# A residual block on one core: the last image's second results stay in SBUF for the last stage, and the involution's constant part is split in two

## The chip, the cores and the metric

The kernel runs on one core of a Trainium2 chip. The metric is device time in microseconds of one execution, the median of several. A profile is one further execution recorded by the hardware profiler. It gives the span from the first to the last instruction of the program, each instruction's start and end, and what the DMA engines moved. Five engines work side by side: TensorE (PE; PEld is its weight load), VectorE (DVE), ScalarE (ACT), GpSimd (POOL) and SyncE (SP). SP and ACT both issue DMA transfers here, SP the loads and most stores, ACT the stores of the output. Each of them takes its instructions in order.

## The reference

The input x has 8 images of 256 channels and 56 x 56 pixels in float32. Two residual layers follow each other:

```
x = x + involution(groupnorm(x))      # 7x7 kernels made from the image itself, 16 groups
y = groupnorm(x)
y1 = conv3x3(y, t(w1)) + conv1x1(y, centre of t(w1))    # t(): weights rounded to -1, 0, 1
r1 = relu(batchnorm(y1))              # mean and variance over all 8 images
y2 = conv3x3(r1, t(w2)) + conv1x1(r1, centre of t(w2))
out = x + relu(r1 + batchnorm(y2))
```

Both batch norms need sums over all images, so each convolution must be complete before the next step can use its result.

## The kernel before, in words

**Involution.** An image is cut into four quarters of 64 channels, 32 quarters in all, and a quarter into ten rows (`TY`), nine of three pixel lines and a last shorter one. While `apply_row` (L905) multiplies the rows of one quarter with its matrices of kernels, `generate` makes the matrices of the next quarter, in 14 units (`UNITS`, L867): TensorE into PSUM, then ScalarE (L871) and VectorE (L881) into SBUF with a bias. `PER_ROW` (L63) says how many steps of the generator follow each row. After the units, `constant` (L819 to L848) adds the part that the group norm's shift contributes: for each of the three pixel lines of a row (`py` 0, 1, 2) and for the last, shorter row (`py` = `PY`, which uses the same reduced image `kr[0]` as line 0) matmuls with summed weights (L832), one activation (L840) and one addition onto x (L847, on GpSimd). It has two steps, of lines (0, 1) and of (2, last row), and both stand in row 8. GpSimd also adds each row's result onto x (L922) and fills the rims of the loaded patches `q` two rows ahead (L797). `reduce` (L759) makes `kr` for the next image in the rows that `STRIPS` names, of the third and fourth quarter. `pin()` holds each engine to the order of the text in this stage. x after the involution goes to DRAM (`x1_d`).

**Convolutions.** `conv_phase` runs twice, over 16 half images. Each half image is transformed along its rows into six planes, split into a high and a low part; TensorE multiplies the planes in the order 1, 2, 3, 4, 0, 5 (`ORDER`, L561) and VectorE combines the results into the half image `y` (tile of two buffers, 12,544 bytes in each partition), whose sums are taken by ScalarE (L491). `y` is stored to DRAM (`y1_d`, then `y2_d`, L605 to L607). The last half image's sums are taken piece by piece so that the batch norm's scale and shift (L186 to L205) follow TensorE's end closely. The weights of planes 1 to 4 lie in the pool `wqa`, those of 0 and 5 in `wqb`.

**Last stage.** 16 tiles (8 images, two tiles of 128 channels), L1152 to L1165. For each tile y1, y2 and x1 are loaded from DRAM by SP (L1160), ScalarE normalizes y1 (L1161), VectorE adds the scaled y2 (L1162), ScalarE applies the relu (L1163), VectorE adds to x1 (L1164) and ACT's queue stores to the output (L1165). The last two tiles go in 2 and 4 parts. The loads may begin before the second convolution has ended, where their memory has been given up. Their memory is four pools, each of which begins where the convolutions' pools lay: y1 and y2 have two buffers each, x1 three, and a pool holds up to three of them. Apart from the involution, the order on an engine comes from a scheduler, which works from the text, the pools and its own estimates.

Of the kernel before, what the change touches and what calls it, by code (L numbers as in the profile page):

```python
# [8 lines left out]
F32 = mybir.dt.float32  # L9
F32R = mybir.dt.float32r  # L10
# [5 lines left out]
SBUF = bass.MemoryType.SB  # L16
# [43 lines left out]

FIRST = (1, 4, 7, 10)

PER_ROW = (2, 2, 2, 1, 2, 2, 1, 2, 2, 0)  # L63
NQB = 5
PLEAD = 2
RIM_AT = 1
# [19 lines left out]
QS = WT  # L86
SLOT = (0, 2, 3, 4, 5, 1)
QM, QM2 = 6, 12


@with_exitstack
def involution_tri_block_kernel(
# [256 lines left out]

    def weights(i, k):  # L350

        w = (wqb if k in ORDER[4:] else wqa).tile([P, CT, 3, C], F32R, tag=f"wq{k}",
                                                  name=f"wq{i}_{k}")
        n = CT * 3 * C
        nc.sync.dma_start(w.rearrange("p t k o -> p (t k o)").bitcast(F32),
                          wq_d[i - 1][:, SLOT[k] * n:(SLOT[k] + 1) * n])
        return w
# [9 lines left out]
            raws.append(raw)  # L367
        return raws

    def conv_phase(i, begun, src_d, norm, stats, shift, dst_d, follow):  # L370

# [154 lines left out]
        for n in range(2 * B):  # L528
            b, h = n // 2, n % 2
            cur, nxt = nxt, {}  # L530
            more = n + 1 < 2 * B
            steps = transform(n + 1, raws, nxt) if more else iter(())
            next(steps, None)
            final = n == 2 * B - 1
            if n + 2 < 2 * B:
                raws = load(i, n + 2, src_d)
            elif not final and follow:
                begun = {}, load(i + 1, 0, dst_d)
            y = wk.tile([P, CT, NH], F32, tag="y", bufs=2, name=f"y{i}_{n}")
            yr = [y.rearrange("p o (r k w) -> p o k r w", k=4, w=W)[:, :, k] for k in range(4)]  # L540

            def row_of(k, x, c, z, op):
                for to in range(CT):
                    nc.vector.scalar_tensor_tensor(yr[k][:, to], x[:, to], c, z[:, to],
                                                   ALU.mult, op)

            def half(name):
                return wk.tile([P, CT, HT, W], F32, tag=name, name=f"{name}{i}_{n}")

            m = {}  # L550
            for k in ORDER:
                ps = ps_c.tile([P, CT, 512], F32, tag="conv", name=f"c{i}_{n}_{k}")
                steps_ = [(to, part, t) for to in range(CT) for part in cur[k] for t in range(CT)]
                if n == 0 and k == 1:
                    steps_ = [(to, part, t) for t in range(CT) for to in range(CT)
                              for part in cur[k]]
                count, last = [0] * CT, CT * 3 * 2 - 1
                for to, part, t in steps_:
                    for dx in range(3):
                        c = count[to]  # L560
                        nc.tensor.matmul(  # L561
                            ps[:, to, :NM], wq[k][:, t, dx, to * P:(to + 1) * P],
                            part[:, t, :, dx:dx + W], start=(c == 0), stop=(c == last))
                        count[to] += 1
                if final and follow:
                    begun[0][k] = weights(i + 1, k)
                m[k] = ps[:, :, :NM].rearrange("p o (r w) -> p o r w", w=W)
                next(done, None)
                if k in (2, 4):
                    e = half("e")  # L570
                    nc.scalar.copy(e, m[k])
                if k == 2:
                    s, d = half("s"), half("d")
                    nc.vector.tensor_tensor(s, m[1], e, ALU.add)
                    nc.vector.tensor_tensor(d, m[1], e, ALU.subtract)
                elif k == 4:

                    s2, d2 = half("s2"), half("d2")
                    nc.vector.tensor_tensor(s2, m[3], e, ALU.add)
                    nc.vector.tensor_tensor(d2, m[3], e, ALU.subtract)  # L580
                    nc.vector.tensor_tensor(yr[1], d2, d, ALU.subtract)  # L581
                    row_of(2, s2, 2.0, s, ALU.subtract)
                    for z, z2, c in ((s, s2, 0.5), (d, d2, 4.0)):
                        flat, flat2 = (v.rearrange("p o r w -> p (o r w)") for v in (z, z2))
                        nc.vector.scalar_tensor_tensor(flat, flat2, c, flat,
                                                       ALU.mult, ALU.subtract)
                    if final:
                        last_rows(n, y, 1, 2)
                elif k == 0:
                    row_of(0, m[0], 1.5, s, ALU.add)  # L590
                    if final:
                        moments = half("s2").rearrange("p o r w -> p o (r w)")[
                            :, :, :18].rearrange("p o (n s) -> p o n s", s=6)
                        row_stats(moments, y, 0, 0)
                elif k == 5:
                    if final:
                        batch_norm_before(stats, total)
                    row_of(3, m[5], 6.0, d, ALU.add)
                    if final:
                        row_stats(moments, y, 3, 1)  # L600
                        row_sums(moments)
                next(steps, None)
            for _ in steps:
                pass
            for to in range(CT):  # L605
                (nc.scalar if final else nc.sync).dma_start(
                    dst_d[b][to][:, h * NH:(h + 1) * NH], y[:, to])  # L607
            done = statistics(n, y)
        return begun, total

# [9 lines left out]
    with ExitStack() as ph1:  # L620
# [198 lines left out]
        def constant(b, c):  # L819
# [1 line left out]
            n = (TY - 1) * TX  # L821
            xv = xs[b, c][:, :(TY - 1) * PY * W].rearrange("p (t y w) -> p y t w", y=PY, w=W)
            scale, bias = prm[b][0][:, c, 1:2], prm[b][2][:, c:c + 1]
            for i0 in (0, 2):
                ps = ps_pair(f"ks_{b}_{c}_{i0}")
                add = work.tile([P, 2 * PX * n], F32, tag="add", name=f"add_{b}_{c}_{i0}")
                for i in range(2):
                    py = (i0 + i) % PY
                    k0, m = (0, n) if i0 + i < PY else (NT, TX)
                    rows = slice(i * CR, (i + 1) * CR)  # L830
                    for h in range(2):
                        nc.tensor.matmul(ps[i][h * CH:(h + 1) * CH, :PX * m], wsx[rows, c, :],  # L832
                                         kr[py][rows, :, k0 + h * m:k0 + (h + 1) * m],
                                         start=True, stop=True)
                for i in range(2):
                    py = i0 + i
                    m = n if py < PY else TX
                    v = add[:, i * PX * n:i * PX * n + PX * m].rearrange(
                        "p (t w) -> p t w", w=W)
# [10 lines left out]
        def generate(b, c, a, shared=()):  # L850

            whole, rest = (v.rearrange("q t (g p) -> q g p t", g=GQ) for v in views(a))
            for u, (gp, p0, n) in enumerate(UNITS):
                ps = ps_pair(f"pg_{b}_{c}_{u}")
                nt = NT + (NE if p0 < PX else 0)
# [25 lines left out]
                        ps[0][:NQ, t0 * n:t1 * n].rearrange("q (t p) -> q t p", p=n),  # L883
                        bt[:, c, g, p0:p0 + n].unsqueeze(1).to_broadcast([NQ, t1 - t0, n]), ALU.add)
                yield
            yield from constant(b, c)

        def apply_row(b, c, a, ty):

# [207 lines left out]

    with ExitStack() as ph2:  # L1100
        rawp, wqa, wqb, pad, tmpp, planes, wk, ps_c = (
            ph2.enter_context(tc.tile_pool(name=name, bufs=bufs, space=space))
            for name, bufs, space in (
                ("rawp", 1, SBUF), ("wqa", 1, SBUF), ("wqb", 1, SBUF), ("pad", 1, SBUF),
                ("tmpp", 1, SBUF),
                ("planes", 8, SBUF), ("wk", 1, SBUF), ("ps_c", 4, PSUM)))

# [11 lines left out]

        xp = pad.tile([P, 4, CT, HT + 1, WP], F32, tag="xp", name="xp")  # L1120
        nc.gpsimd.memset(xp.rearrange("p f t r w -> p (f t r) w")[:, :, ::WP - 1], 0.0)
        begun, total = conv_phase(1, begun, x1_d, norm_x1, st1, nc1, y1_d, True)

# [7 lines left out]
                nc.vector.tensor_scalar(dst, src, scale, bias, ALU.mult, ALU.add)  # L1133
                nc.vector.tensor_scalar(dst, dst, 0.0, None, ALU.max)

        _, total = conv_phase(2, begun, y1_d, norm_y1, st2, nc2, y2_d, False)

    sc2, bi2 = batch_norm_params(total, nc2, g2_sb, b2_sb, "bn2")  # L1140
    with ExitStack() as ph4:

        fa, fb, fc, fd = (ph4.enter_context(tc.tile_pool(name=name, bufs=1))
                          for name in ("fa", "fb", "fc", "fd"))
        homes = {"y1": (fd, fa), "y2": (fd, fb), "x1": (fd, fb, fc)}

        def home(name, j):
            k = j % len(homes[name])
            return homes[name][k].tile([P, HW], F32, tag=f"{name}{k}", name=f"{name}f_{j}")


        for j in range(B * CT):  # L1152
            b, t = j // CT, j % CT
            y1f, y2f, x1f = (home(name, j) for name in ("y1", "y2", "x1"))
            n = {B * CT - 2: 2, B * CT - 1: 4}.get(j, 1)
            f = HW // n
            for cols in (slice(k * f, (k + 1) * f) for k in range(n)):
                y1, y2, x1 = y1f[:, cols], y2f[:, cols], x1f[:, cols]
                for v, src in ((y1, y1_d), (y2, y2_d), (x1, x1_d)):
                    nc.sync.dma_start(v, src[b][t][:, cols])  # L1160
                nc.scalar.activation(y1, y1, AF.Relu, bias=bi1[:, t:t + 1], scale=sc1[:, t:t + 1])  # L1161
                nc.vector.scalar_tensor_tensor(y1, y2, sc2[:, t:t + 1], y1, ALU.mult, ALU.add)  # L1162
                nc.scalar.activation(y1, y1, AF.Relu, bias=bi2[:, t:t + 1])  # L1163
# [88 lines left out]
```

## Time and profile before

| what | us |
|---|---|
| median of three runs | 2143.46 (2142.48 to 2144.44) |
| profiled execution, its own time | 2144.3 |
| its span | 2142.5 |
| involution, 58 to 1035 us of the span | 977 |
| first convolution, 1035 to 1478 | 443 |
| second convolution, 1478 to 1908 | 430 |
| after TensorE's end, 1908 to 2142.5 | 234.5 |
| TensorE busy over the span | 1750.4 (82%) |
| VectorE busy over the span | 1760.6 (82%) |
| ScalarE busy over the span | 1428.7 (67%) |
| GpSimd busy over the span | 584.1 (27%) |

The stages' limits are read from the times at which TensorE's lines change. A busy share over the whole span mixes stages of different kinds, so the prediction reads each stage by itself. In a group of instructions the last column gives the idle time of the engine just before them and what ended it; in the DMA view a queue's bytes and the mean rate count.

### The profile page before, as it was taken

Reading aid. Unit: us, or ns where it says so; the run is one execution under the profiler, and the core shown is the slowest. Engines: PE = TensorE matmul, PEld = TensorE weight load, DVE = VectorE, ACT = ScalarE, POOL = GpSimd, SP = SyncE. Lnnn points to the kernel's source line nnn. Section 1 sums busy time; section 2 is a strip of 40 time slices with the busy share of each in tenths; the row PEclk is TensorE's granted clock in tenths of the full one; section 3 lists DMA queues with packets and bytes.
Section 4 is the critical chain, followed back from the end, with each engine's and each line's share of the span. In section 5 each row is a group of like instructions: output and inputs, shape, how many; then the busy total and the mean of one; then the engine's idle time right before and its main releaser. Section 6 shows DMA issues by size and latency. Waiting matters only on the chain.

```text
span 2142.5 us, 70728 instructions
## 1 busy us (share of the span) xinstructions
PE 1750.4 (82%) x29680; PEld 1621.5 (76%) x29680; DVE 1760.6 (82%) x3360; ACT 1428.7 (67%) x3537; POOL 584.1 (27%) x960
## 2 busy tenths in 40 slices
PE   5898898989898897988799999998999999960000
PEld 5787777868777686877799999998999999950000
DVE  6778879787777878777899999998999999984444
ACT  4877787877778687777466666665676666653343
POOL 1655566555655555565000000000000000000000
PEclk9999999999999899999899999999999999985555
DMA  5767677686757768677633333335333333369999
GB/s 186 235 181 235 208 237 237 198 254 199 254 180 245 223 179 254 180 205 210 235 123 123 123 123 123 123 123 203 112 139 125 120 126 123 122 270 428 430 429 393
DMA packets 155370, 440.06 MB, mean 205 GB/s; under 512 B 63006, under 2 KB 73116, under 8 KB 147628
## 3 DMA queue, kind: packets, MB, share of 16 engines
q1 hardware_dynamic: 149760, 403.89, 55.2%
q10 hardware_dynamic: 5004, 31.56, 3.5%
q8 instruction: 235, 3.85, 0.7%
q14 instruction: 83, 0.68, 0.1%
q0 software_dynamic: 288, 0.08, 0.0%
HBM read 323.28 MB, written 112.20 MB: 203 GB/s over the span
## 4 chain that ended last, share of the span: by engine, by line
PE 69%; DVE 11%; DMA 9%; issue 5%; ACT 4%; POOL 1%; SPq 0%; ACTq 0%; POOLq 0%; DVEq 0%
PE c L561 39%; PE pg L867 15%; PE pa L905 9%; PE pk L759 4%; DMA y1f<-y1d 3%; DMA x1f<-x1d 2%; ACT a L871 2%; PE ks L832 2%; DMA out_y<-x1f 2%; DMA y2f<-y2d 1%; DVE inv L917 1%; DVE x1f L1164 1%; DVE a L881 1%; DVE st L153 1%; ACT add L840 1%
## 5 line engine op out<-in xcount | busy, mean ns | idle before, releaser
L561 PE MATMUL c<-pl,wq 128*128 128x392 f32 x4608 | 858.0, 349 | 11.3 <-ACT pl L433 9.2
L561 PEld LDWEIGHTS c<-pl,wq 128*128 128x128 f32 x4608 | 855.1, 190 | 13.9 <-ACT pl L433 9.6
L871 ACT ACTIVATE a<-pg,bt 126x126 f32<-126x126 f32 x2028 | 524.8, 457 | 110.8 <-PE pg L867 110.5
L867 PE MATMUL pg<-kr,wl 64*126 64x140 f32 (+1 forms) x6144 | 456.3, 291 | 43.2 <-ACT a L871 17.3
L867 PEld LDWEIGHTS pg<-kr,wl 64*126 64x126 f32 x6144 | 395.3, 194 | 72.7 <-issue 28.5
L905 PE MATMUL pa<-a,q 126*32 126x48 f32 x17024 | 289.0, 215 | 63.7 <-issue 55.6
L905 PEld LDWEIGHTS pa<-a,q 126*32 126x32 f32 x17024 | 241.1, 116 | 128.9 <-issue 86.8
L881 DVE TENSOR_TENSOR a<-pg,bt 126x504 f32<-126x504 f32 (+4 forms) x640 | 280.8, 481 | 37.4 <-PE pg L867 35.9
L922 POOL TENSOR_TENSOR x<-x,inv 128x168 f32<-128x168 f32 x310 | 161.1, 520 | 394.9 <-DVE inv L917 355.4
L917 DVE SCALAR_TENSOR_TENSOR inv<-pa,gn1s,inv 128x168 f32<-128x168 f32 (+1 forms) x384 | 134.0, 351 | 156.3 <-ACT inv L915 153.4
L410 ACT CAST pl<-r 128x812 fp32r<-128x812 f32 x190 | 160.7, 868 | 130.8 <-DVE r L405 121.5
L386 POOL MEMSET xp<- 128x116 f32 x32 | 6.3, 196 | 828.4 <-DVE a L405 805.1
L797 POOL TENSOR_TENSOR q<-q,sides 126x256 f32<-126x256 f32 (+1 forms) x320 | 225.7, 706 | 7.8 <-DMA q<-in_x_nb 7.8
L411 DVE TENSOR_TENSOR pl<-r,pl 128x812 fp32r<-128x812 f32 x190 | 185.3, 1002 | 28.0 <-ACT pl L410 26.7
L491 ACT ACTIVATE dummy<-y,nc 128x1568 f32<-128x1568 f32 (+1 forms) x128 | 200.2, 1564 | 4.8 <-DVE y L581 3.5
L915 ACT ACTIVATE inv<-pa,gn1s 128x168 f32<-128x168 f32 x320 | 133.3, 417 | 62.8 <-PE pa L905 47.6
L153 DVE BATCH_NORM_STATS2 st<-x 128x6 f32<-128x392 f32 x256 | 138.0, 555 | 7.9 <-DMA x<-in_x 7.4
L847 POOL TENSOR_TENSOR x<-x,add 128x504 f32<-128x504 f32 x124 | 123.2, 1024 | 12.6 <-ACT add L840 12.6
L1131 ACT ACTIVATE xp<-raw,bi_bn,sc_bn 128x392 f32<-128x392 f32 (+1 forms) x125 | 83.0, 721 | 60.3 <-DVE a L405 58.9
L1111 ACT ACTIVATE xp<-raw,gn 128x392 f32<-128x392 f32 (+1 forms) x125 | 83.3, 721 | 52.7 <-DVE a L405 51.6
L1162 DVE SCALAR_TENSOR_TENSOR y1f<-y2f,sc_bn,y1f 128x3136 f32<-128x3136 f32 (+2 forms) x20 | 56.6, 2831 | 62.8 <-DMA y2f<-y2d 52.5
L759 PE MATMUL pk<-x,wrn 64*128 64x168 f32 (+1 forms) x1152 | 101.8, 317 | 0.1
(186 smaller groups left out, 1812.0 us busy)
## 6 DMA issues: line engine op xcount, KB each, us to landing
q<-in_x_nb SPq DMA_DIRECT2D x320, 448.0 KB, 4.2
raw<-x1d SPq DMA_DIRECT2D x32, 812.0 KB, 7.0
raw<-y1d SPq DMA_DIRECT2D x32, 812.0 KB, 5.9
x1d<-x SPq DMA_DIRECT2D x64, 392.0 KB, 5.2
x<-in_x SPq DMA_DIRECT2D x60, 392.0 KB, 5.2
y1d<-y SPq DMA_DIRECT2D x30, 784.0 KB, 3.3
y2d<-y SPq DMA_DIRECT2D x30, 784.0 KB, 3.8
y1f<-y1d SPq DMA_DIRECT2D x14, 1568.0 KB, 15.1
```

The costliest lines, as they stand in the source:

```text
L153: nc.vector.bn_stats(st[:, j, :], xt[:, j * NC:(j + 1) * NC])
L410: nc.scalar.copy(hi, r)
L411: nc.vector.tensor_tensor(lo, r, hi.bitcast(F32), ALU.subtract)
L491: nc.scalar.activation(dst, v, f, bias=shift[:, to:to + 1], accum_out=stats[:, to, j, n:n + 1])
L561: nc.tensor.matmul(ps[:, to, :NM], wq[k][:, t, dx, to * P:(to + 1) * P], part[:, t, :, dx:dx + W], start=(c == 0), stop=(c == last))
L759: nc.tensor.matmul(ps[h][:, :m * W], wrn[rows, c, :], src[rows, r0:r0 + (m - 1) * PY + 1:PY, :], start=(c == 0), stop=(c == NCQ - 1))
L797: nc.gpsimd.tensor_tensor(v, v, z, ALU.add)
L867: nc.tensor.matmul(dst, wl[rows, c, gp, o:o + NQ], kr[py][rows, px, :], start=True, stop=True)
L871: nc.scalar.activation(dst[:, g + 1, p0 + j], ps[1][:NQ, j * nt + t0:j * nt + t1], AF.Identity, bias=bt[:, c, g + 1, p0 + j:p0 + j + 1])
L881: nc.vector.tensor_tensor(dst[:, g, p0:p0 + n].rearrange("q p t -> q t p"), ps[0][:NQ, t0 * n:t1 * n].rearrange("q (t p) -> q t p", p=n), ...
L905: nc.tensor.matmul(ps[o:o + m, k * w:(k + 1) * w], q[:NQ, k, o:o + m], av[:, t + k, g * w:(g + 1) * w], start=True, stop=True)
L922: engine.tensor_tensor(xv, xv, iv.rearrange("p t (y x) -> p y t x", x=PX), ALU.add)
```

## The change

Five edits, in two places of the program.

- **Second results that stay.** `conv_phase` gets an argument `stays`. In the second convolution the two half images of the last image are not stored; their tiles `y` are kept. So that they outlive the convolution's pools, `y` moves to a pool `keep` on the other side of SBUF, opened ahead of the convolutions.
- **The last stage opens with the last image.** Tile j belongs to image (j / 2 - 1) mod 8. Tiles 0 and 1 take y2 from the kept half images, in two parts each, and load y1 and x1 alone. Ten loads are written ahead of the loop, in the order of `FIRST_LOADS`.
- **Pools of the last stage.** Eleven pools, one to a tile: four buffers for y1, two for y2, four for x1, and one spacer (`SPACE`), so that each tile lies over few of the convolution's pools. y1's first buffer lies over none of them.
- **Weights in three pools**, of two planes each in the order of use: 1 and 2, 3 and 4, 0 and 5.
- **The constant part in two halves.** The pairs are now (0, last row) and (1, 2). The first stands after the sixth unit (`CONST_AT`), in row 3; the second stays in row 8. `PER_ROW` changes so that row 3 has no unit and row 6 has two.

In the built program SP issues y1 tile 0's load at the start of the second convolution, between the weight loads and the raw loads of half image 1. The order of the next loads on SP is y1 tile 1, x1 tile 1, y1 tile 2, x1 tile 0, y2 tiles 2 and 3, x1 tile 2, y1 tile 3, x1 tile 3. ScalarE's first activations of y1 tiles 0 and 1 stand inside the second convolution, and that of y1 tile 2 ahead of the last four sums.

```diff
-PER_ROW = (2, 2, 2, 1, 2, 2, 1, 2, 2, 0)
+PER_ROW = (2, 2, 2, 1, 2, 2, 2, 2, 1, 0)
+CONST_AT = 5
...
+FIRST_LOADS = [("y1", 0), ("y1", 1), ("x1", 1), ("x1", 0), ("y1", 2), ("y2", 2), ("y2", 3),
+               ("x1", 2), ("y1", 3), ("x1", 3)]
...
-        w = (wqb if k in ORDER[4:] else wqa).tile([P, CT, 3, C], F32R, tag=f"wq{k}",
+        w = wqs[ORDER.index(k) // 2].tile([P, CT, 3, C], F32R, tag=f"wq{k}",
...
-            y = wk.tile([P, CT, NH], F32, tag="y", bufs=2, name=f"y{i}_{n}")
+            y = keep.tile([P, CT, NH], F32, tag="y", bufs=2, name=f"y{i}_{n}")
...
-            for to in range(CT):
-                (nc.scalar if final else nc.sync).dma_start(
-                    dst_d[b][to][:, h * NH:(h + 1) * NH], y[:, to])
+            if stays is not None and b == B - 1:
+                stays.append(y)
+            else:
+                for to in range(CT):
+                    (nc.scalar if final else nc.sync).dma_start(
+                        dst_d[b][to][:, h * NH:(h + 1) * NH], y[:, to])
...
-            for i0 in (0, 2):
+            for pair in ((0, PY), (1, 2)):
...
+            made = constant(b, c)
             for u, (gp, p0, n) in enumerate(UNITS):
...
                 yield
-            yield from constant(b, c)
+                if u == CONST_AT:
+                    next(made)
+                    yield
+            yield from made
...
+    keep = ctx.enter_context(tc.tile_pool(name="keep", bufs=1, side="right"))
...
-        fa, fb, fc, fd = (ph4.enter_context(tc.tile_pool(name=name, bufs=1))
-                          for name in ("fa", "fb", "fc", "fd"))
-        homes = {"y1": (fd, fa), "y2": (fd, fb), "x1": (fd, fb, fc)}
+        h = [ph4.enter_context(tc.tile_pool(name=f"f{i}", bufs=1)) for i in range(11)]
+        h[9].tile([P, SPACE], F32, tag="space2", name="space2")
+        homes = {"y1": (h[10], h[0], h[4], h[7]), "y2": (h[6], h[2]),
+                 "x1": (h[5], h[1], h[3], h[8])}
...
+        for name, j in FIRST_LOADS:
+            tail_load(name, j)
         for j in range(B * CT):
-            b, t = j // CT, j % CT
...
+            b, t = (j // CT - 1) % B, j % CT
+            n = parts_of.get(j, 1)
             f = HW // n
...
+            for k in range(n):
+                cols = slice(k * f, (k + 1) * f)
+                for name in ("y1", "y2", "x1"):
+                    if (name, j) not in FIRST_LOADS and (name != "y2" or j >= CT):
+                        tail_load(name, j, cols)
+                y1, x1 = (tiles[name, j][:, cols] for name in ("y1", "x1"))
+                y2 = stays[k][:, t] if j < CT else tiles["y2", j][:, cols]
```

## The prediction

> **What bounds the kernel now.** I read the slices of the page first, then busy time by stage, then inside the two stages that the change touches. In the slices (each digit a tenth of busy share, the span cut into 40) TensorE is busy to slice 36 and the DMA engines only after it:
>
> ```profile
> PE   5898898989898897988799999998999999960000
> DVE  6778879787777878777899999998999999984444
> DMA  5767677686757768677633333335333333369999
> ```
>
> Busy time by stage follows: involution, first convolution, second convolution, last stage. Columns: stretch, its length, then PE, PEld, DVE, ACT and POOL busy, granted clock, DMA share, GB/s.
>
> ```profile
> 58.00:1035.00 977.00, 856.46 (x24612) 733.35 (x24608) 774.73 (x2143) 744.09 (x2652) 566.83 (x907) 0.95 0.72 221
> 1035.00:1478.00 443.00, 430.30 (x2308) 428.25 (x2308) 421.25 (x552) 282.73 (x385) 3.13 (x16) 0.99 0.37 137
> 1478.00:1908.00 430.00, 428.64 (x2304) 427.66 (x2304) 411.14 (x505) 282.97 (x376) 2.93 (x15) 0.99 0.35 130
> 1908.00:2142.50 234.50, 0.00 (x0) 0.00 (x0) 115.57 (x62) 92.58 (x43) 0.00 (x0) 0.50 0.99 417
> ```
>
> The convolutions are TensorE (428.6 of 430 us). The last stage is DMA: share 0.99, 417 GB/s, VectorE half idle. Its waits (who waited for whom: total us, times, longest) all end in a transfer, first or at one remove:
>
> ```profile
> ACT y1f L1161 <- DMA y1f<-y1d: 68.6, 16, 10.7
> ACT y1f L1163 <- DVE y1f L1162: 61.9, 18, 5.6
> DVE y1f L1162 <- DMA y2f<-y2d: 52.5, 14, 5.2
> DVE x1f L1164 <- DMA out_y<-x1f: 28.1, 7, 4.2
> ```
>
> The DMA view over 1892 to 2140 us gives the bytes:
>
> ```profile
> DMA packets 11856, 104.01 MB, mean 419 GB/s; under 512 B 1312, under 2 KB 1312, under 8 KB 4812
> ```
>
> So the last stage costs bytes over rate, and it begins when its loads can begin. That is set by when the second convolution gives up SBUF. The timeline shows the last half image leave its planes: plane 2 evacuated at 1889.53 (so weights 1, 2 are free), plane 4 at 1898.33 (3, 4 free), plane 5 at 1907.21 (0, 5 free).
>
> ```profile
> 1889.53 0.82 ACT L571 COPY e<-c 128x784 f32<-128x784 f32 x1 [1.75 <-PE c L561]
> 1898.33 0.81 ACT L571 COPY e<-c 128x784 f32<-128x784 f32 x1 [2.16 <-PE c L561]
> 1907.21 1.04 DVE L544 SCALAR_TENSOR_TENSOR y<-c,d 128x392 f32<-128x392 f32 x2 [0.48 <-PE c L561]
> ```
>
> The involution has no single bound: PE is busy 856 of 977 us. Groups from 58 to 1035 us (busy, mean ns | idle before, releasers):
>
> ```profile
> L905 PE MATMUL pa<-a,q 126*32 126x48 f32 x16072 | 256.5, 214 | 63.7 <-issue 55.6 <-POOL q L797 4.8 <-DVE inv L917 2.5
> L867 PE MATMUL pg<-kr,wl 64*126 64x140 f32 x1968 | 163.6, 302 | 29.2 <-ACT a L871 17.1 <-DVE a L881 10.8 <-PE pa L905 0.7
> L847 POOL TENSOR_TENSOR x<-x,add 128x504 f32<-128x504 f32 x92 | 113.9, 1265 | 0.0
> L840 ACT ACTIVATE add<-ks,gn1b,gn 128x504 f32<-128x504 f32 x93 | 65.1, 768 | 12.2 <-PE ks L832 12.0
> ```
>
> Most of PE's idle time there (55.6 us) has no releaser; 17.1 us wait for ScalarE to empty PSUM, 4.8 for POOL to fill rims.
>
> [...] 429 to 430 in each 50 us stretch from 1950 to 2100. [...] here SP's loads (76.8 MB) and ACT's stores (27.2) add up to that one rate. [...] a load at SP's head that waits for a buffer holds up what is behind it. The trace agrees: at 1926 us the third x1 load waits until 1933.17, and the next y1 load until 1946.01.
>
> **The last stage, counted in moves.** One move is 128 x 3136 x 4 B = 1.606 MB: 3.73 us at 430 GB/s.
> - Before: y1 tile 1 was loaded at 1868.47. From 1890.6 on remain 15 y1, 16 y2, 16 x1 and 16 out, plus the y2 stores of half images 14 and 15 (two halves each, one move per half image): 65 moves, 104.4 MB, which is what the view shows. They end at 2141: 250.4 us, 3.85 us a move with start and end losses in it.
> - Removed: both y2 loads of image 7 and both y2 moves of its half images (4 moves).
> - Moved: y1 tile 0 has its own pool in space that y left, so the built order puts its load on SP at the start of convolution 2, ahead of the raw loads of half image 1. One move less: 60 remain.
> - Start: the second load (x1 tile 1) lies in weights 1, 2, now a pool of their own: issued at 1889.5 instead of 1890.6. Behind it y1 tile 2 (about 1890), x1 tile 0 and y2 tile 2 (about 1892), y2 tile 3 (1898.3), then x1 tile 2 at PE's end, 1907.2, with two more loads queued behind it. Five moves are 18.7 us of work from about 1891, so the engines run dry near 1909.7; the load issued at 1907.2 comes in time, barely. Three moves carry on to about 1921.
> - First store: the batch norm ends at 1912.4; a half of 1568 takes 1.85 + 1.85 (VectorE does both halves of tile 0 first), then 1.6 ScalarE and 1.79 VectorE: about 1918, against 1922.8. So stores join before the loads run out.
> - Sum: 60 x 3.85 = 231.1 from 1889.5 is 2120.6, against 1890.6 + 250.4 = 2141.0: **-20.4 us**. The other way: 60 x 3.735 = 224.1, a start of 1.5 and the end loss of 5 (379 against 430 GB/s over the last 43 us) give 2120.1, plus 0 to 3 us of gaps such as those near 1922 (339 GB/s). Bounds -18 to -22; I take -20.5.
>
> **Costs inside the convolutions.** The early y1 load: the y1 store of the last half image, which it waits for, lands at 1476.6; raw tile 1 was issued at 1475.92 anyway. Two raw loads then land some 4 us later than 1480.8 and 1483.8; ScalarE first reads one at 1487.1, VectorE the planes at 1493.4, and PE has work until 1505 (1478.5 + 428.6 / 16). Hidden: 0, at most 4. The relus of y1 tile 0 (2 x 1.7 us) now run inside convolution 2, where ScalarE is 66% busy: 0. ScalarE has y1 tile 2's relu (3.0 us) ahead of the last four statistics, which the batch norm needs; if its load lands by 1900 the statistics end near 1908, before VectorE's own 1909.1; if it came 3 us late the norm would be 2 us late, under cover of three queued loads. Three weight pools, the loop from image 7 and y on the other side of SBUF issue nothing more: 0.
>
> **The involution.** Matmuls, activations and adds of the constant part are the same in number; only pairs and places change. Before, row 8 of a quarter carried all of it: 2.2 us of PE, four activations, and a POOL burst of 3 x 1.27 + 0.30 = 4.1 us. After, row 3 has one large and one small part (POOL 1.57), row 8 two large (2.53). For it the one unit of row 3 goes to row 6, so rows 4 to 7 have two units each. Gain: POOL's burst delays the rims of rows 9 to 1; of 4.8 us of PE waits for rims (and 13.8 on the weight-load side) perhaps 3 go, and a PSUM pair less is held at row 8 (5.6 us of weight-load idle). POOL is idle 1.5 to 2 us in each of rows 3 to 6, so its share of row 3 is covered. Loss: with no light row at 6 ScalarE may fall behind; a row of two units takes PE 0.80 + 2.03 us (timeline) and ScalarE 2.4 (eight activations that start 0.25 us apart and one of 0.43), so PE still sets the pace. No trace shows the new order: -12 (all 4.8 us for POOL and a quarter of the 28 us for PSUM gone) to +20 (0.65 us for each of 31 quarters). I take -3.
>
> **Total.** The profiled execution has a span of 2142.5 and a time of 2144.3; the median shown is 2143.5. 2143.5 - 20.5 - 3 = **2120**.
>
> **Rivals.**
> - A, as above: 2115 to 2125. Chance 0.58.
> - B, the opening runs dry: x1 tile 2 at SP's head waits for PE's end while two ready loads stand behind it, or the stores join late; 4 to 8 us of gap, 2125 to 2132. For it: the margin at 1909 is under 1 us. Against: stores join before 1921. 0.16.
> - C, the involution gains more, since the burst had spread into the unnamed idle time: 7 to 12 us, 2108 to 2115. Against it: gaps without a releaser also stand in the middle of a row, where POOL has no part. 0.14.
> - D, the involution pays: in rows 4 to 7 PE waits for ScalarE to free PSUM, as it did 16 times for 17.1 us (1.07 each) in rows 1 and 2. Once in each of 31 quarters is 33 us: 2143.5 - 20.5 + 33 = 2156, slower. It decides from 0.66 us a quarter (20.5 / 31). 0.12, of which 0.03 stays faster and 0.02 within the bound.
> - That y2 still went through DRAM is excluded: the built order has no load or store of it for image 7.
>
> **Range and chances.** 0.2% (4.3 us) is about what can be told from no change. Faster: 0.58 + 0.16 + 0.14 + 0.03 = 0.91; same 0.02; slower 0.07. 2109 to 2132 takes in A, B and most of C, and leaves D and C's end.
>
> **What would show it.** The last stage's bytes fall by 8 MB at an unchanged 430 GB/s; DMA share is near 1 from 1890 with no dip at 1909 or 1922 (a dip there is B); the first store is near 1918 on before's clock; convolution 2 keeps its 430 us (more means that the early load cost). The involution ends 0 to 8 us earlier with fewer waits of L905 for POOL; L867 waiting for ScalarE in rows 4 to 7 is D. A last stage shortened by less than 15 us without a dip would make the count of moves wrong.

## The result and the profile after

The changed kernel takes 2127.78 us (median of 15 executions, 2117.0 to 2142.0) against 2144.6 us for the kernel before, run beside it (15 executions, 2135.05 to 2159.61). The ratio is 0.9916, 95% interval 0.9897 to 0.9934: 18 us less by the ratio, 17 by the medians. The forecast was 2120 us, 23.5 less. The last stage gained what was forecast; some 6 us of the whole gain are missing.

The profiled execution has a span of 2127.9 us, 14.6 below the span before. In the slices the last four are DMA alone, as before; in the slice ahead of them TensorE is now busy for 9 tenths instead of 6:

```profile
PE   5898898989989798988799999997999999990000
DMA  5667677686767858676733333336233333349999
```

The stretches of involution, second convolution and last stage follow (length, then PE, PEld, DVE, ACT, POOL busy, granted clock, DMA share, GB/s):

```profile
58.00:1035.00 977.00, 859.10 (x24634) 729.14 (x24628) 774.84 (x2142) 741.20 (x2653) 566.90 (x906) 0.94 0.72 221
1478.00:1908.00 430.00, 424.16 (x2272) 423.02 (x2273) 406.22 (x498) 281.85 (x375) 2.93 (x15) 0.98 0.34 129
1913.00:2127.90 214.90, 1.16 (x7) 0.81 (x5) 116.91 (x69) 90.65 (x45) 0.00 (x0) 0.51 0.99 419
```

After TensorE's end the last stage is still DMA at a share of 0.99 and 419 GB/s, and it takes 213.7 us where it took 235.3. The second row tells what went wrong. In its 430 us TensorE did 2272 of the convolution's 2304 matmuls; before, all 2304 fitted (1.2 us of this is a later start). From first matmul to last end, the second convolution grew from 428.6 to 434.4 us.

**Where the 5.8 us went.** The chain of work that ended last, of the kernel after (three of its pieces in a row, with start, duration, engine or transfer), passes through the early load of y1 tile 0:

```profile
1471.18 6.65 DMA y1d<-y
1477.84 6.51 DMA y1f<-y1d
1488.13 426.04 PE c L565 x2292
```

The timeline of the same moments (start, duration, idle time before and what ended it), first before and then after, shows how a load gets in TensorE's way:

```profile
1478.54 21.81 PE L561 MATMUL c<-pl,wq 128*128 128x392 f32 x106 [9.24 <-ACT pl L433]
1481.13 0.53 ACT L433 CAST pl<-r 128x406 fp32r<-128x406 f32 x1 [2.64 <-DVE r L432]
```

```profile
1477.84 0.32 SPq L1172 DMA_DIRECT2D y1f<-y1d  x1
1479.78 4.29 PE L565 MATMUL c<-pl,wq 128*128 128x392 f32 x12 [9.24 <-ACT pl L437]
1484.38 3.28 ACT L1187 ACTIVATE y1f<-y1f,bi_bn,sc_bn 128x1568 f32<-128x1568 f32 x2 [4.65 <-DMA y1f<-y1d]
1487.57 0.51 ACT L437 CAST pl<-r 128x406 fp32r<-128x406 f32 x1
1488.13 27.14 PE L565 MATMUL c<-pl,wq 128*128 128x392 f32 x137 [4.06 <-ACT pl L437]
```

On ScalarE the first activation of y1 tile 0 (L1187) stands ahead of a cast (L437) that makes a plane of half image 0. ScalarE waits 4.65 us for the load, then works 3.28 us on it (two activations), and only then makes the cast. TensorE has done the 12 matmuls it could do and waits 4.06 us for that cast. Before, the same cast (L433) began 2.6 us after the first matmul, under cover of the 12, and TensorE ran on.

The gap is not the whole loss: the clock also comes up later. Stretches of 1 us show it (same columns; the clock is the third number from the end), two of before:

```profile
1482.00:1483.00 1.00, 1.00 (x5) 1.00 (x4) 1.00 (x3) 0.87 (x1) 0.00 (x0) 0.52 0.39 162
1483.00:1484.00 1.00, 1.00 (x7) 0.99 (x6) 1.00 (x2) 0.00 (x0) 0.00 (x0) 1.00 0.02 7
```

and four of after:

```profile
1483.00:1484.00 1.00, 1.00 (x4) 0.55 (x2) 1.00 (x2) 0.00 (x0) 0.00 (x0) 0.50 0.86 359
1484.00:1485.00 1.00, 0.07 (x1) 0.00 (x0) 1.00 (x2) 0.62 (x1) 0.00 (x0) 0.50 1.00 422
1491.00:1492.00 1.00, 1.00 (x5) 1.00 (x4) 1.00 (x2) 0.95 (x2) 0.00 (x0) 0.62 0.00 0
1492.00:1493.00 1.00, 1.00 (x8) 1.00 (x7) 1.00 (x2) 0.96 (x2) 0.00 (x0) 1.00 0.00 0
```

Before, the clock rises from 0.50 to 1.00 at about 1483.0, 4.4 us after the stage's first matmul. After, it is still at 0.50 when the gap comes, 4.3 us after the first matmul, stays there through the gap, and rises at about 1491.8 (a mean of 0.62 in that microsecond), 3.6 us after the gap. At 0.50 TensorE works at about half rate: the 12 matmuls ahead of the gap took 4.29 us, 0.36 us each, where the 2304 of before's stage took 428.6 us, 0.19 each in the mean (the counts of a 1 us stretch take in matmuls that reach over its limits). So it works at that rate for 4.3 + 3.6 = 7.9 us instead of 4.4. By these two rates the 3.5 us more lose some 1.7 us, an estimate, and 4.06 + 1.7 = 5.8 us, the growth of the stage. What brings the clock up is not shown: before, it came 4.4 us after the first matmul; after, 4.3 us of work ahead of the gap had not brought it.

**The last stage.** Its first loads go out as plane 2 is done, and the first store follows TensorE's end by 10.5 us (timeline of after):

```profile
1896.46 0.32 SPq L1172 DMA_DIRECT2D x1f<-x1d  x1
1896.52 0.81 ACT L575 COPY e<-c 128x784 f32<-128x784 f32 x1 [1.75 <-PE c L565]
1914.20 1.04 DVE L548 SCALAR_TENSOR_TENSOR y<-c,d 128x392 f32<-128x392 f32 x2 [0.49 <-PE c L565]
1924.67 2.12 ACTq L1191 DMA_DIRECT2D out_y<-x1f  x2
```

The DMA view of after over 1896 to 2127 us has 7.6 MB less than that of before over 1892 to 2140 us; both windows leave out a little at either end:

```profile
DMA packets 11236, 96.38 MB, mean 417 GB/s; under 512 B 1248, under 2 KB 1248, under 8 KB 4832
```

From the load at 1896.46 to the landing of the last store (2126.4) are 230.0 us; 60 moves at 3.85 us were to take 231.1. What shifted is the start, by 7.0 us: 5.8 from the second convolution, and 1.2 from a second convolution that began 1.2 us later.

**The involution.** TensorE's waits by name, of the kernel after, over 58 to 1035 us (total us, times, longest):

```profile
PE pa L914 <- issue: 65.4, 54, 5.4
PE pg L873 <- issue: 18.6, 14, 3.9
PE pg L873 <- ACT a L877: 10.8, 12, 2.1
PE pg L873 <- DVE a L887: 5.2, 8, 1.0
```

The waits for ScalarE and VectorE to empty PSUM fell from 17.1 and 10.8 us, and the wait for GpSimd's rims, 4.8 us before, is gone. But idle time without a releaser ("issue") grew, and the stretch from the first to the last row takes 974.9 us against 975.1. One profile of each can't tell whether the involution gained.

### The profile page after: what moved, and what is told of

It reads as the page before. It is cut to its first block, busy times and chain, and to the rows that moved or that the text cites. A ratio compares the mean times of both kernels' runs of the same rounds, so it can differ in the third digit from the quotient of the medians.

```text
span 2127.9 us, 70742 instructions
## 1 busy us (share of the span) xinstructions
PE 1755.5 (82%) x29680; PEld 1618.6 (76%) x29680; DVE 1762.0 (83%) x3364; ACT 1426.1 (67%) x3541; POOL 584.1 (27%) x960
## 3 DMA queue, kind: packets, MB, share of 16 engines
q8 instruction: 235, 3.85, 0.8%
## 4 chain that ended last, share of the span: by engine, by line
PE 72%; DMA 11%; DVE 9%; issue 5%; ACT 3%; ACTq 0%; POOL 0%; SPq 0%; DVEq 0%
PE c L565 39%; PE pg L873 16%; PE pa L914 10%; DMA y1f<-y1d 7%; PE pk L766 4%; PE ks L838 2%; ACT a L877 1%; DMA out_y<-x1f 1%; DVE a L887 1%; DVE st L157 1%; DVE inv L926 1%; DMA wqd<-piece_w 1%; DMA wr<-in_w_red 1%; DVE y1f L1188 1%; DVE piece_w L320 0%
## 5 line engine op out<-in xcount | busy, mean ns | idle before, releaser
L877 ACT ACTIVATE a<-pg,bt 126x126 f32<-126x126 f32 x2028 | 516.9, 452 | 93.1 <-PE pg L873 92.6
L873 PE MATMUL pg<-kr,wl 64*126 64x140 f32 (+1 forms) x6144 | 447.5, 291 | 35.7 <-issue 18.6
L845 ACT ACTIVATE add<-ks,gn1b,gn 128x504 f32<-128x504 f32 (+1 forms) x128 | 80.3, 681 | 30.0 <-PE ks L838 28.5
```

The costliest lines, as they stand in the source:

```text
L873: nc.tensor.matmul(dst, wl[rows, c, gp, o:o + NQ], kr[py][rows, px, :], start=True, stop=True)
L877: nc.scalar.activation(dst[:, g + 1, p0 + j], ps[1][:NQ, j * nt + t0:j * nt + t1], AF.Identity, bias=bt[:, c, g + 1, p0 + j:p0 + j + 1])
```

## The experiments

Four questions: is it the place of the activation on ScalarE or the early load itself that cost 5.8 us; what is the constant part worth; what is a move worth; and what are the gaps without a releaser. The kernels of e1 to e4 ran beside the kernel before on one chip (2155.61 us there), e5 to e8 on another occasion (2151.63), e9 and e10 on a third (2151.08). The kernels' executions scatter by some 8 us either way, so comparisons of times go by ratios and their intervals, and stages are read from the profiles.

### e1_relu_held and e2_load_late: the activation or the load

e1 keeps the load where it is, and only orders the first activation of y1 tile 0 behind ScalarE's work on half image 13 (no wait is added, only a place in the order):

```diff
+            if stays is not None and n == 2 * B - 3:
+                for ins in nc.cur_bb.bb.instructions:
+                    late[ins.engine] = ins
...
                 nc.scalar.activation(y1, y1, AF.Relu, bias=bi1[:, t:t + 1], scale=sc1[:, t:t + 1])
+                if j == 0:
+                    hold(nc.cur_bb.bb.instructions[-1])
```

> The first activation of y1 tile 0 is held behind the sums of half image 13 on ScalarE; its load stays where it is, ahead of the raw loads. Theory (ScalarE takes its instructions in order, and the activation that waits for the load stands ahead of the cast that TensorE needs): TensorE's gap of 4.06 us and the slow clock after it go, convolution 2 takes 430 us again instead of 435, and everything after it moves up by 6 to 7 us: about 24 us under the kernel before (ratio 0.989) against 17 to 18 of the changed kernel. Rival (the load itself is at fault, since it delays the raw loads of half image 1): a gap of about 4 us in TensorE at the start of convolution 2 stays, and the time is that of the changed kernel (ratio 0.992).

e2 does the same and also puts the load itself behind the store of half image 13 on SP:

```diff
         for name, j in FIRST_LOADS:
             tail_load(name, j)
+            if (name, j) == ("y1", 0):
+                hold(nc.cur_bb.bb.instructions[-1])
```

> As the run with the held activation, and the load of y1 tile 0 is held too, behind the second results of half image 13 on SP, when the DMA engines are idle. Theory: the same as with the activation alone held, within 1 us (ratio 0.989), since the early load costs nothing that TensorE sees and a load at 1870 us is still outside the crowded stretch. Rival (the load is at fault): only here does TensorE's gap go, 6 us less than with the activation alone held.

Measured: e1 2124.84 us (2119.26 to 2136.83), ratio 0.9871 (0.9841 to 0.9901); e2 2124.83 us (2120.44 to 2127.66), ratio 0.9864 (0.9841 to 0.9888). In e1's timeline the load still goes out 1.9 us before the first matmul, and TensorE runs on without a gap:

```profile
1490.13 0.32 SPq L1183 DMA_DIRECT2D y1f<-y1d  x1
1492.01 28.27 PE L573 MATMUL c<-pl,wq 128*128 128x392 f32 x141 [9.23 <-ACT pl L445]
```

The activations of y1 tiles in e1 (duration min/median/max, first and last start) now begin 390 us later:

```profile
L1198 ACT ACTIVATE y1f<-y1f,bi_bn,sc_bn x5: 1688/1704/3012, 1883.4 to 1914.9; 128x1568 f32<-128x1568 f32 x4, 128x3136 f32<-128x3136 f32 x1
```

The second convolution is back at 428.6 us in e1 and 428.8 in e2, with no gap over 0.15 us. So the place of the activation cost the 5.8 us; the early load costs nothing that shows, as e1, which keeps it, takes no longer than e2. That the load delays the raw loads and so the planes, the rival, falls.

### e3_tail_only and e4_const_only: each half of the change alone

e3 is the changed kernel with the constant part and `PER_ROW` of before; e4 is the kernel before with the new ones. Of e4's edit:

```diff
-PER_ROW = (2, 2, 2, 1, 2, 2, 1, 2, 2, 0)
+PER_ROW = (2, 2, 2, 1, 2, 2, 2, 2, 1, 0)
+CONST_AT = 5
...
-            for i0 in (0, 2):
+            for pair in ((0, PY), (1, 2)):
...
+            made = constant(b, c)
...
-            yield from constant(b, c)
+                if u == CONST_AT:
+                    next(made)
+                    yield
+            yield from made
```

> The changed kernel with the involution of the kernel before (constant part in one row, old steps per row). If the involution's edit is worth nothing in time, as the two profiles say (first to last row 974.9 and 975.1 us): the changed kernel's time, 17 to 18 us under before (ratio 0.992). If it is worth the 3 us of the prediction: 14 to 15 us under before (0.9935). If it costs: under 0.990.

> The kernel before with the involution of the changed kernel alone. Worth nothing: ratio 1.000. Worth the 3 us of the prediction: 0.9985. In its profile TensorE's waits for POOL (4.8 us before) are near 0 and those for PSUM fall from 28 to about 16, as in the changed kernel; the first to the last row takes 975 us if gaps without a releaser take their place, 963 if they do not.

Measured: e3 2136.18 us (2125.64 to 2146.78), ratio 0.9913 (0.9881 to 0.9946), with the same gap of 4.0 us and a second convolution of 434.4 us. e4 2146.84 us (2135.06 to 2150.03), ratio 0.9947 (0.992 to 0.9975): 11 us less, 5 to 17. Each is faster than the kernel before, but the two do not add up: together they would make 30 us, and the whole change makes 18. e3's ratio leaves nothing for the constant part, since the changed kernel itself has 0.9916 and, run again in e5, 0.9909. e4's last stage is that of before (234.9 us after TensorE's end), so a gain can only lie in the involution, and there the waits fell much as expected, those for GpSimd to none and those for PSUM to 18.8 us (about 16 expected). Yet the involution of e4's profiled execution takes 980.0 us, 5 more than before's; 963 or 975 had been expected.

### e5_after_again, e6_two_weight_pools, e7_four_more_moves: what the last stage's parts are worth

e5 is the changed kernel once more:

> The changed kernel itself, beside the next runs on one chip. Theory (last stage -21, blocked cast +7, involution 0 to -6): 14 to 20 us under before, ratio 0.9905 to 0.9935; TensorE's gap of about 4 us at the start of convolution 2 is there again. If the involution's edit were worth the 11 us of its own run: ratio 0.988.

2129.57 us (2125.06 to 2139.56), ratio 0.9909 (0.9882 to 0.9936); its profile has the gap again (4.24 us). The result repeats.

e6 is e2 with the weights in two pools, planes 1 to 4 and 0, 5:

```diff
-        w = wqs[ORDER.index(k) // 2].tile([P, CT, 3, C], F32R, tag=f"wq{k}",
+        w = wqs[ORDER.index(k) // 4].tile([P, CT, 3, C], F32R, tag=f"wq{k}",
...
```

> As the run with load and activation held, but the weights in two pools as before (planes 1 to 4, planes 0 and 5). The scheduler then puts x1 tile 1 behind x1 tile 0 on SP, where it waits for plane 4. Theory (DMA sets the last stage, and it starts with the first load that gets through): y1 tile 2 opens at about 0.6 us later than x1 tile 1 did, x1 tile 1 waits 9 us for plane 4 under cover of two loads of 7.5 us; from TensorE's end to the span's end 214 to 216 us instead of 213.5. Rival (the third pool carries the early start): 222 us, 9 us more.

2131.38 us (2123.16 to 2134.35), ratio 0.9901 (0.9872 to 0.9929). The last stage takes 214.1 us from TensorE's end, against 213.5 in e2, as the theory had it. By these two profiles the third pool is worth about 0.6 us there; the ratios, 0.9901 against 0.9864 in e2 and 0.9876 in e10, lie further apart, and only the scatter of executions is known to account for that.

e7 is e2 with four more loads in the last stage, of x1 into the spacer, whose contents nobody reads:

```diff
+        spare = h[9].tile([P, SPACE], F32, tag="space2", name="space2")
...
+                if 6 <= j < 10:
+                    nc.sync.dma_start(spare[:, (j - 6) * HW:(j - 5) * HW], drams["x1"][b][t][:, :])
```

> As the run with load and activation held, and four more loads of 1.606 MB in the middle of the last stage, into the spare space, used by nobody: as many moves as the change took out by keeping y2. Theory (bytes over rate): from TensorE's end to the span's end 213.5 + 4 x 3.73 to 3.85 = 228.4 to 228.9 us. Rival (the last stage is bound by waits for buffers between the loads, not by bytes): under 222 us.

2139.34 us (2128.73 to 2145.62), ratio 0.9943 (0.9917 to 0.9968). The stretch from TensorE's end to the end of the span in e7:

```profile
1913.10:2142.90 229.80, 0.00 (x0) 0.00 (x0) 116.20 (x67) 90.22 (x44) 0.00 (x0) 0.51 0.99 418
```

and in e2:

```profile
1908.10:2121.50 213.40, 0.00 (x0) 0.00 (x0) 116.11 (x67) 89.33 (x42) 0.00 (x0) 0.51 0.99 419
```

229.8 - 213.4 is 16.4 us for four moves, 4.1 us each, at the same share and rate and with the same work on VectorE and ScalarE. That is some 1 us more than was expected (228.4 to 228.9), and far from the rival's 222. A move costs its bytes, at the price that the prediction used (3.85) or a little more.

### e8_more_traffic: what the gaps without a releaser are

TensorE's idle time without a releaser is the largest part of its idle time in the involution: 69.6 us before, 85.8 after. The DMA view lists a queue of the kind "instruction", q8, that moves 235 packets of 16 KiB in an execution (3.85 MB, 0.7% of the 16 engines' time before, 0.8% after), 195 of them in the involution. Of the 66 such gaps of before, 58 (66.0 of the 69.6 us) end 1.2 to 1.7 us after the end of one of these packets, of the 71 after, 62 (77.4 of 85.8 us); a moment drawn at random does so in one of ten cases. Some two thirds of the 195 packets have no such gap behind them. Whose instructions q8 moves, the trace does not say; that TensorE waits in these gaps for its own is the author's conjecture.

If the gaps are fetches that come late, more data traffic ought to lengthen them. e8 is e2 with one more transfer in each row of the involution, 224 KB from DRAM to DRAM, which nobody reads:

```diff
+EXTRA = 448
...
+            to = dram.tile([P, EXTRA], F32, tag="more", bufs=4, name=f"more_{b}_{c}_{ty}")
+            r0 = (HQ - QY - PY * ty) * QX
+            nc.sync.dma_start(to, x_nb[b, c, r0:r0 + P, :EXTRA])
...
+                more_traffic(b, c, ty)
```

> As the run with load and activation held, and in each row of the involution one more transfer of 224 KB from DRAM to DRAM, which nobody waits for but its own buffer. Theory (TensorE's gaps without a releaser in the involution are waits for its own instructions, which come through the same DMA engines): these gaps, 85 us in the four profiles with the new order, grow beyond 110 us and the involution by as much, while waits for loaded patches stay small. Rival (the gaps have nothing to do with DMA): they stay within 70 to 95 us and the involution within 973 to 988 us.

2176.34 us (2175.02 to 2184.97), ratio 1.0129 (1.0096 to 1.0162). The involution of e8, and TensorE's waits in it:

```profile
58.00:1080.00 1022.00, 878.00 (x24610) 744.34 (x24609) 769.11 (x2133) 746.01 (x2647) 566.77 (x906) 0.93 0.87 279
```

```profile
PE pa L932 <- issue: 90.1, 79, 4.0
PE pg L891 <- issue: 27.1, 23, 2.5
PE pg L891 <- ACT a L895: 7.3, 8, 1.7
PE pa L932 <- DMA x<-in_x: 1.0, 1, 1.0
```

With the DMA share at 0.87 instead of 0.73 (e2), the gaps without a releaser grow from 85.0 us (e2) to 118.8, and 99 of 105 follow a packet of instructions at the same distance. Waits for data hardly appear (1.0 us for x), and waits for ScalarE and VectorE fall. That the gaps are late instruction fetches is supported, by place and by response. No run takes the fetches away, so it is not shown.

The involution grew by 48 us, the gaps by 34. The waits for other engines fell by 10 us, and TensorE's busy time grew by 24 (857 to 881 us from the first to the last row) with the same matmuls. Much of that is the clock: it stood at 0.50 for 151 us of that stage instead of 102. A matmul of a row takes 282 ns at 0.50 and 209 ns at 1.00, and over the eleven other profiles of this case TensorE's busy time in the stage, 846 to 866 us, rises by 0.3 us for each us at 0.50 (70 to 132 us; correlation 0.95). By that, an estimate, the clock makes 15 of the 24 us; the rest stays open.

### e9_old_rows_held and e10_held_again: the constant part once more

e9 is e2 with the constant part and `PER_ROW` of before, that is, e2 with e3's edit; e10 is e2 unchanged.

> The changed kernel with the late load and the held activation of e2_load_late, but with the constant part and the rows of the kernel before. It leaves no part of the computation out. Against e10_held_again, which differs from it in the involution alone, the prediction's -3 us for the constant part gives a time 3 us longer here; the comparison in e4_const_only (a ratio of 0.9947 against the kernel before) gives 11 us longer; a constant part that moves nothing gives the same within 3 us. In the trace, whatever the time, waits of the piece matmuls for GpSimd of 4 to 7 us and waits of the kernel generator's matmuls for ScalarE and VectorE of 25 us or more should be back. Convolution 2 as in e2_load_late: 428.6 to 428.9 us without a gap; last stage 213 to 215 us from TensorE's end.

> e2_load_late unchanged, beside e9_old_rows_held on one chip. A ratio to the kernel before of 0.984 to 0.989 if what e2_load_late showed holds.

e9 2131.44 us (2121.36 to 2135.19), ratio 0.9898 (0.9874 to 0.9922); e10 2123.47 us (2115.29 to 2135.13), ratio 0.9876 (0.9847 to 0.9906). The kernel with the new constant part is 8 us faster by the medians, 5 by the ratios; the intervals overlap, so this can be nothing too. e9's second convolution takes 428.7 us, as expected, and its last stage 215.6, 0.6 above the range. In e9's waits the rims are back:

```profile
PE pa L922 <- POOL q L814: 5.2, 6, 1.6
PE pg L884 <- ACT a L888: 12.2, 13, 2.4
PE pg L884 <- DVE a L898: 9.0, 8, 2.1
```

The waits for PSUM came back less than was expected: 21.2 us instead of 25 or more, against 17.2 in e10:

```profile
PE pg L884 <- ACT a L888: 12.5, 13, 2.1
PE pg L884 <- DVE a L898: 4.7, 7, 1.4
```

Over all profiles but e8's, TensorE's idle time in the involution is, in us (gaps over 0.15 us, from the traces):

| constant part | profiles | for VectorE, ScalarE, GpSimd | without a releaser | both |
|---|---|---|---|---|
| as before | before, e3, e9 | 45 (37 to 53) | 75 (70 to 82) | 121 (117 to 127) |
| in two halves | after, e1, e2, e4, e5, e6, e7, e10 | 31 (28 to 34) | 84 (78 to 94) | 116 (109 to 123) |

14 us of named waits go, 9 us come back as gaps without a releaser, about 5 us stay. The two groups of named waits do not overlap; the sums do. And TensorE's busy time does not stay the same beside them: it is 855 us in the mean with the old rows and 861 with the new, with the clock at 0.50 for 87 and for 116 us. That takes back the 5 us. Whether the new rows bring the clock down or these profiles happen to differ, three profiles against eight can't tell. The involution's length itself is 973 to 978 us with the old rows and 969 to 988 with the new, so the profiles do not show a gain in it.

## Why the prediction was right, and where it failed

**The last stage, counted in moves: right.** From its first load to the landing of its last store 230.0 us were measured and 231.1 predicted, with 60 moves at an unchanged rate; the first store came 10.5 us after TensorE's end, which is 1917.7 on before's clock, where 1918 was predicted. e7 priced a move at 4.1 us where 3.85 was taken. From TensorE's end the stage is 21.6 us shorter, where 20.5 was predicted from the first load's time. Of the five moves that went, the four of y2 are worth some 16 us by e7's price; the moved load and the earlier start make up the rest.

**Rival B, the opening runs dry: not seen.** The rate was 420 to 433 GB/s from 1900 to 1916, 379 in the 4 us after that and 386 from 1924 to 1928; the forecast's place for a dip, 1909 on before's clock, is 1916 here, and 10 to 12% of two stretches of 4 us is about 1 us. The other place, 1922, is 1929 here: 405 GB/s from 1928 to 1932, where before had 339. The time measured, 2127.8 us, lies in the band that the prediction gave to B (2125 to 2132) and not in its own (2115 to 2125), yet B did not happen. That the whole range held owes this much to luck.

**"The relus of y1 tile 0 (2 x 1.7 us) now run inside convolution 2, where ScalarE is 66% busy: 0": this step failed.** It took a mean over 430 us for a place. Beside it, "PE has work until 1505" took half image 0 for work that lies ready; in fact ScalarE and VectorE make its planes as TensorE goes, and after 12 matmuls TensorE needs the cast that began at 1481.13 before. The order built for ScalarE put the activation at the one point where TensorE had a supply of 12 matmuls and nothing behind it, and the activation waited for a load issued 6.5 us before. The prediction had seen that the built order issues this load at the start, and asked what the load delays on SP, but not what the instruction that needs it delays on ScalarE. Price: 4.65 us of wait and 3.28 us of work on ScalarE made a gap of 4.06 us on TensorE, and the clock that came up later 1.7 us more: 5.8 us. e1, which moves the activation alone, gets it back.

**The early y1 load, "Hidden: 0, at most 4": right.** e1 has it and its second convolution takes 428.6 us. The sign that the prediction gave (a convolution longer than 430 us "means that the early load cost") would have led to the wrong instruction: it was longer, and the load did not cost.

**"Three weight pools … issue nothing more: 0": right as a cost.** As a gain of start the third pool brings about 0.6 us (e6), less than the 1.1 us that the forecast took for the earlier first load.

**The involution, -3 us: not settled.** The waits went as its steps had it: GpSimd's 4.8 us to 0, PSUM's 28 us to 16. Whether time was gained is less clear. Three comparisons of times give -11 (e4 with before, 5 to 17), -5 to -8 (e10 with e9, within the noise) and 0 (the changed kernel with e3, within the noise). The profiles give 5 us less idle and 6 us more busy time. The last two and the profiles agree with -3; e4's interval lies beyond it, and e4 alone shows a sign. What was not foreseen is that TensorE, freed from one wait, meets another: two thirds of what was removed came back without a releaser. e8 supports that this is the supply of instructions, but no run removes it, so why it takes back these two thirds stays open. Rival C (a gain of 7 to 12 us) would fit e4, and by the medians e10 with e9; e3 and the profiles speak against it, and no run excludes it.

**Rival D, TensorE waits for ScalarE in rows 4 to 7: refuted.** Over the whole involution those waits fell from 17.1 us to 10.8, and D would have needed 20 us more of them to undo the gain of the last stage.

**The sum.** -21.6 for the last stage, 0 to -8 for the involution and +5.8 for the second convolution give -16 to -24, against -17 to -18 measured (-14 to -22 by the interval). Without the misplaced activation, e1, e2 and e10 measure ratios of 0.9864 to 0.9876, 27 to 29 us below the kernel before. That is some 9 us under the changed kernel's own ratio, where 5.8 would be the stage's growth; e2's interval alone lies clear of the changed kernel's.

## What to carry to other kernels

When work of a later stage is let into an earlier one, look in the built order at what stands behind each instruction that waits for a transfer, on its own engine, and at how much work the next engine has ready at that moment; a low mean busy share (66% of ScalarE here) says nothing of that place. A stage at its DMA rate can be forecast by counting equal moves and timing the start (here 231.1 us for the 230.0 measured). Where an engine is short of several things at once, waits taken away by name can come back in part under another (here 14 us went and 9 us came back), so price such a gain by the engine's whole idle time, and look at its busy time too, which here changed with the clock.

## What the runs showed of the hardware that was not expected

- A gap of 4.06 us on TensorE cost 5.8. It came 4.3 us after the stage's first matmul, with the clock still at 0.50, and the clock rose 3.6 us after the gap; without a gap it rose 4.4 us after the first matmul.
- TensorE's busy time for the same matmuls of the involution was 846 to 881 us over the profiles, the longer the more time the clock stood at 0.50 (70 to 151 us).
- TensorE's gaps without a releaser, 63 to 105 in the involution and 1.0 to 1.3 us each, mostly end about 1.4 us after a 16 KiB packet of the queue q8, kind "instruction" (58 of 66 before, 62 of 71 after), and grew from 85 to 119 us when the DMA share went from 0.73 to 0.87.
- Executions of one kernel on one chip spread over 7 to 25 us (2117.0 to 2142.0 for the kernel after), and the involution of the kernels with the new rows over 969 to 988 us, so that the profile of one execution could not tell a gain of 5 us there.
